# Two fused image layers on one core: half of the first image's sums by 32 x 32 block transposes, a new scratch layout, and output products on tiles of 32 rows and 64 columns

## The chip, the cores and the metric

The kernel runs on one core of a Trainium2 chip. The metric is the device time of one execution, in microseconds (us); the runs before the change are summed up by their median.

## The reference

The input x has 8 images of 256 channels and 96 x 96 pixels, fp32. Two layers are applied one after the other, each with a residual:

```python
# --- layer 0: attention over channels, in the frequency domain ---
x = x + L0(_gn(x))
#   q, k, v = fft2(1x1 conv of _gn(x)), 8 heads of 32 channels
#   attn = q_normalized . k_normalized * temperature      (over all frequencies)
#   out = |ifft2((softmax(real attn) + i softmax(imag attn)) . v)|, then a 1x1 conv
# --- layer 1: linear attention over pixels ---
x = x + L1(_gn(x))
#   q = softplus(Wq x + bq), k = softplus(Wk x + bk), v = Wv x + bv
#   out = q . (k v^T) / (q . sum k)
```

Sums over all frequencies of products of two transforms are sums over pixels, so the kernel never transforms whole images: it needs the channel covariance of each image with itself and with its mirror image (row -h, column -w), and a rotated copy of the image for the imaginary part.

## The kernel before, in words

One program works on the 8 images one after the other, as generators that are interleaved by hand: each `yield` is a place where another generator may put its instructions, and within each engine the order of the program is the order of execution (`tc.manual_schedule`). Two SBUF arenas hold the current image x (`x_of(b)`) and its rotated copy y (`y_of(b)`); the next image's x uses the arena of the current y.

Per image b there are these stages:

- **Sums** (`first_sums` for image 0, `pair_sums` for the others). A pair of image rows and its mirrored rows are transposed so that pixels lie on partitions; `pair` makes the sum e and the difference o of the two; `products` multiplies e and o with themselves, 8 matmuls per product step, accumulated in two PSUM tiles `acc`. `first_sums` mirrors rows on ScalarE (`mirrored`, L394), transposes them on PE (`turn`, L410), copies them out of PSUM (L412) and takes 96 pixels of one row per product step: 24 units of two steps, and the middle row. The transposed rows stay in SBUF at hand-chosen `places`. `pair_sums` loads the image with 32 channel groups on partitions (`load_grouped`: DMAs of 192 KB into 32 partitions each), turns 32 x 32 blocks on VectorE (`turn_blocks`, L510), makes e on GpSimd (L537) and o on VectorE or GpSimd (L538), and takes 128 pixels per product step: 12 units of three steps, and the middle row. Its transposed rows are written to the DRAM scratch `xtd` (L515), a group of two units with one DMA; the middle row goes to `xtm`.
- **Attention and rotation** (`attention`, `rotate`, joined by `mix`). `attention` is a long chain of small steps from the covariance to the table mz; `rotate` makes y by products of the transposed rows with a table of shifted sines (`tm`, read from `rx` in DRAM), 49 steps in all, whose matmuls stand at L128 in the helper `in_halves` as `y<-tm,arena`. `fetch` brings a block of transposed rows back from `xtd` (L799), or, for image 0, finds it at its place. `mix` puts one rotation step at each yield of the chain.
- **Images** (`images`): reloads x, applies mz to y (L875), takes squares and roots, projects with wo (L884) and adds to x. Beside it the next image's sums run (`weave`).
- **Layer 1** (`layer1`, `output`). `output` selects the reciprocal denominators (`select`, L1135), multiplies (L1146), makes the output products (L1173) from 32-row slices, adds them to x (L1178 on VectorE; L1181 and L1182 through ScalarE and GpSimd) and stores the image (L1186). Beside it run the end of the next image's sums and its first 16 rotation and chain steps.

All DMAs are issued by SP in program order. The helper that splits a product into two tiles of 64 columns:

```python
def in_halves(out, lhsT, rhs, start, stop):
    for h in halves:
        nc.tensor.matmul(out[h], lhsT=lhsT[:, h], rhs=rhs, start=start, stop=stop, skip_group_check=True)
```

What orders the work around the change: for image 0, `first_sums` runs to its end with table set-up steps (`tables`) put in from its 11th yield and rotation steps from its 16th, then `mix`; for the others `weave` adds up the yields' numbers and takes one step of the sums each time the sum passes 1. Rings bound how far an engine runs ahead: five `ring` tiles for e and o, five PSUM tiles `ps`, three `acc`.

Of the kernel before, what the change touches and what calls it, by code (L numbers as in the profile page):

```python
# [74 lines left out]
def two_layer_kernel(ctx: ExitStack, tc: tile.TileContext, x, w1t, b1, w2t, b2, w3, b3, wot, temp,  # L75
# [58 lines left out]
    TO = 2 * SG + 4  # L134

# [4 lines left out]
    def turned(b):  # L140

        return [x_of(b)[:, c, TO:TO + 2 * NQ * C].rearrange("p (q r n) -> p q r n", q=NQ, r=2) for c in range(2)]
# [70 lines left out]
    def load_small():  # L213
# [16 lines left out]
        for j in range(16):  # L230
            nc.sync.dma_start(out=wo[NH * j:NH * j + NH, 1, :], in_=wo_v[HEAD - j if j else 16])
            if j % 4 == 3:
                yield
# [17 lines left out]
    xtd = dram.tile([2, NG // 2, P, 2 * NQ * C], F32, name="xtd")  # L251
# [89 lines left out]
    def release(key):  # L341
        if next(held.get(key, iter(())), None) is None:
# [4 lines left out]
              *((0, k, o) for k, o in ((0, 1280), (0, 2304), (0, 5888), (0, 6912), (1, 5888), (1, 6912))),  # L347
              *((1, k, 0) for k in range(KC)), *((0, 1, o) for o in (1280, 2304)), *((1, k, o) for o in (8192, 1024, 7168, 2048, 6144, 3072) for k in range(KC))]
# [6 lines left out]
    def first_loads():  # L355

        nc.sync.dma_start(out=t0[:, 0:2 * W], in_=tmat[0, :, W:3 * W])
        x0 = x_of(0)

        def load(lo, hi):  # L360
            nc.sync.dma_start(out=x0[:, :, lo * W:hi * W], in_=x_v[0, :, :, lo * W:hi * W])

        for lo, hi in ((0, 4), (H - 4, H), (4, 8), (H - 8, H - 4), (8, 16), (H - 16, H - 8)):
            load(lo, hi)
        yield
        load(16, 24)
        yield
        for lo in (H - 24, 24, H - 32):
            load(lo, lo + 8)
        yield  # L370
        for t in range(4, NT // 2):
            load(8 * t, 8 * t + 8)
            load(H - 8 * t - 8, H - 8 * t)
        yield

    def first_sums():
# [3 lines left out]
        acc = [acc_tile(f"acc{c}_{b}") for c in range(2)]  # L380
        CB = C + 2
        NU = H // 4
        eos, gs = {}, {}

        xr = x0[:, :, 0:HW].rearrange("p k (h w) -> p k h w", w=W)

        def mirrored(u):

            nr = 2 if u < NU else 1
            g = two.tile([P, CH], F32, tag="v16", name=f"g_{b}_{u}")[:, 0:KC * nr * W].rearrange("p (k r w) -> p k r w", k=KC, r=nr)  # L390
            h = H - 2 * u
            parts = [(g, xr[:, :, h:h - nr:-1])] if u else [(g[:, :, r:r + 1], xr[:, :, (H - r) % H:(H - r) % H + 1]) for r in range(nr)]
# [5 lines left out]
        def turn(u):  # L398

            t = place(u)  # L400
            nr = 2 if u < NU else 1
            g = gs.pop(u)
            if u < NU:
                gs[u + 1] = mirrored(u + 1)
            for c in range(2):
                pt = ps_tile(f"x_{b}_{u}_{c}")
                for r in range(nr):
                    for k in range(KC):
                        v = g[:, k, r, :] if c else xr[:, k, 2 * u + r, :]
# [4 lines left out]
        def pair(u):  # L414

            nr = 2 if u < NU else 1
            eo = ring_tile(f"eo_{b}_{u}")[0:W, 0:2 * nr * CB].rearrange("p (q c n) -> p q c n", q=nr, c=2)
            f, g = (place(u)[:, c * N2:c * N2 + nr * C].rearrange("p (r n) -> p r n", r=nr) for c in range(2))
            e, o = (eo[:, :, c, 1:C + 1] for c in range(2))
            nc.gpsimd.memset(eo[:, :, :, 0:CB:CB - 1], 1.0 if u < NU else R2)  # L420
            if u in (0, NU):
# [5 lines left out]
            if u < NU:  # L427
                nc.gpsimd.tensor_add(e, f, g)
                nc.vector.tensor_sub(o, f, g)
# [7 lines left out]
        for u in range(NU + 1):  # L437
            if u + 2 <= NU:
                turn(u + 2)
            if u < NU:  # L440
                pair(u + 1)
            eo = eos.pop(u)
            for q in range(2 if u < NU else 1):
                products(acc, eo, q, W, u == 0 and q == 0, u == NU)
            yield
        s0[b] = acc, weights(b)
# [25 lines left out]
    def pair_sums(b):  # L472

        ready = {}

        def prepare(key, step):
            if key in (("turn", 10), ("pair", 10), ("turn", 11), ("turn", 12)):
# [8 lines left out]
        acc = [acc_tile(f"acc{c}_{b}") for c in range(2)]  # L486
# [4 lines left out]
        def turn_blocks(u):  # L491

            v, r = divmod(u, 2)
            t = turned(b)
# [19 lines left out]
            if r:  # L514
                nc.sync.dma_start(out=xtd[:, v].rearrange("c p m -> p c m"), in_=x_of(b)[:, :, TO:TO + 2 * NQ * C])  # L515
# [3 lines left out]
        def pair(u):  # L519
# [3 lines left out]
            ft, gt = (t[0:np_, 0:nq, u % 2] for t in turned(b))  # L523
# [17 lines left out]
        finish(turn_blocks(0))  # L541
        finish(make(0))
        finish(turn_blocks(1))
        if b:
            finish(make(1))
        yield
        for u in range(NG + 1):
# [15 lines left out]
    def attention(b):  # L563
# [37 lines left out]
        nmean, rstd, dm = yield from group_norm(mv, f"a{b}", 1)  # L601
# [4 lines left out]
        yield 4  # L606
# [152 lines left out]
    def rotate(b):  # L759
# [5 lines left out]
        def load_r(i):  # L765
# [3 lines left out]
            if b == 0 and i < NP:  # L769
# [8 lines left out]
        assert LO + 16 * C <= AW and LO + 12 * C <= LO + NS * CH + 2 * CH  # L778
        xts, tms = {}, {}
        at_ = [0]  # L780

        def fetch():
# [8 lines left out]
            if b == 0:  # L791
# [5 lines left out]
            else:  # L797
                v, a = divmod(i, G)
                nc.sync.dma_start(out=xts[i], in_=xtd[:, v, 32 * a:32 * a + 32].rearrange("c j (q m) -> (j q) c m", q=NQ))  # L799
# [34 lines left out]
    def images(b):  # L834
# [100 lines left out]
        for p in pending:  # L935
            yield 1
            project(*p)
# [4 lines left out]
    def layer1(b):  # L942
# [4 lines left out]
        nmean, rstd, _ = yield from group_norm(mv, f"b{b}")  # L947
# [182 lines left out]
    def output(b, x, kq, rec, am, columns_of, fetch=None, sums=None, mixed=None):  # L1130

        def select(s, pd, half=2):
            t, g = divmod(s, 4)
            n = slice(CH // 2 if half == 1 else 0, CH if half else CH // 2)
            nc.tensor.matmul(pd[:, n], lhsT=sel8[32 * g:32 * g + 32, t * P:(t + 1) * P], rhs=rec[32 * g:32 * g + 32, n],  # L1135
                             start=True, stop=True, skip_group_check=True)
# [30 lines left out]
        for s in range(NS):  # L1167
            for m in range(KC):
                po = []
                for j in range(NB):  # L1170
                    ps = ps_tile(f"o_{b}_{s}_{m}_{j}")
                    jj = slice(32 * j, 32 * j + 32)
                    nc.tensor.matmul(ps[:, 0:CH], lhsT=am[jj, m * P:(m + 1) * P], rhs=qn(s)[jj], start=True, stop=True)  # L1173
# [26 lines left out]
    def mix(b, chain, turns):  # L1200

        for n in chain:
            for _ in range(n):
                next(turns, None)
                yield
# [6 lines left out]
    with tc.manual_schedule(engines={E.PE, E.DVE, E.Pool, E.SP, E.Activation}):  # L1212
        sums, loads, parts = first_sums(), first_loads(), tables()
# [8 lines left out]
        for i, _ in enumerate(sums):  # L1222
            if i > 9:
                next(parts, None)
            if i > 14:
                next(turns)
        finish(mix(0, attention(0), turns))
# [61 lines left out]
```

## Time and profile before

| what | value |
|---|---|
| runs before | 2467.61, 2470.61, 2471.26 us; median 2470.61 |
| profiled execution | 2469.41 us, of which the span of instructions 2467.6 us |
| PE matmul busy | 2385.8 us (97%), granted clock 0.983 of full |
| PE weight loads busy | 1492.3 us (60%) |
| VectorE (DVE), ScalarE (ACT), GpSimd (POOL) busy | 1782.0 us (72%), 1162.1 us (47%), 864.7 us (35%) |
| DMA | 395.26 MB, mean 160 GB/s; 53.7% of 16 engines' span |

How to read it: busy times are shares of one profiled execution. A row of a group of instructions names the line, the engine, the operation, what it writes and reads, the shape, the count, busy us and mean ns of one, then the engine's idle time just before them and what ended it. Matmuls are pipelined, so a busy PE is not PE at its peak. An fp32 product appears in the trace as two matmuls (two passes), each with its weight load; a transpose as one. A DMA share of 1 means that all 16 engines had a packet in work all the time. Stretches are given as start:end in us from the start of the span.

### The profile page before, as it was taken

The page shows a single profiled execution, that of the slowest core. Times are in us where ns is not written, and L with a number is a line of the kernel's source. Part 1 is how long each engine was busy: PE and PEld are TensorE (multiplying, and loading weights), DVE is VectorE, ACT ScalarE, POOL GpSimd, SP SyncE. Part 2 cuts the span into 40 slices and gives each one's busy share as a digit, 9 for nine tenths or more (in the row PEclk, how much of TensorE's full clock was granted, in tenths as well). Part 3 has the DMA queues.
Part 4 walks back from the last instruction along what each step waited for, and adds up shares of the span by engine and source line. Part 5 has one row for each costly group of instructions (what it writes and reads, how often), then busy time and mean ns, then how long its engine had stood idle before and what let it go on. Part 6 is the DMA issues. An engine that isn't in the chain of part 4 may idle for free. (4 is left out here: it accounts for less than half of the span.)

```text
span 2467.6 us, 60810 instructions
## 1 busy us (share of the span) xinstructions
PE 2385.8 (97%) x25296; PEld 1492.3 (60%) x25296; DVE 1782.0 (72%) x3472; ACT 1162.1 (47%) x2053; POOL 864.7 (35%) x820
## 2 busy tenths in 40 slices
PE   9999998999989999899999999989999999999998
PEld 7854666456774566645666456664666546665446
DVE  4478785688857887578775787757886578866777
ACT  3354354544535445354453535435364453644553
POOL 4124513344213543135331352413524136142311
PEclk9999999999999999899999999999999999999997
DMA  8135729266391755916559263783638737296004
GB/s 234 41 130 128 190 78 329 106 164 155 129 335 53 175 139 167 333 34 160 135 196 316 53 171 96 251 260 65 167 88 297 214 65 200 54 329 207 1 8 154
DMA packets 264718, 395.26 MB, mean 160 GB/s; under 512 B 37400, under 2 KB 194300, under 8 KB 264444
## 3 DMA queue, kind: packets, MB, share of 16 engines
q1 hardware_dynamic: 264444, 391.38, 53.7%
q8 instruction: 200, 3.28, 0.6%
q14 instruction: 74, 0.61, 0.1%
HBM read 246.99 MB, written 144.32 MB: 159 GB/s over the span
## 5 line engine op out<-in xcount | busy, mean ns | idle before, releaser
L875 PE MATMUL z<-arena,mz 128*64 128x384 f32 (+1 forms) x3840 | 594.9, 489 | 0.0
L927 POOL TENSOR_TENSOR e<-e 128x768 f32<-128x768 f32 x192 | 349.7, 1821 | 533.7 <-ACT e L926 507.7
L884 PE MATMUL po<-e,wo 128*64 128x384 f32 x3072 | 529.4, 486 | 1.8 <-ACT e L928 1.8
L875 PEld LDWEIGHTS z<-arena,mz 128*64 128x64 f32 (+1 forms) x3840 | 247.5, 132 | 296.6 <-issue 287.4
L922 DVE TENSOR_TENSOR e<-z,xT 128x768 f32<-128x768 f32 x384 | 359.2, 947 | 43.8 <-PE z L875 43.0
L884 PEld LDWEIGHTS po<-e,wo 128*64 128x64 f32 x3072 | 227.9, 137 | 266.3 <-issue 235.2
L469 PE MATMUL acc<-eo 128*64 128x193 f32 (+6 forms) x4928 | 379.5, 303 | 0.8 <-DVE eo L425 0.4
L469 PEld LDWEIGHTS acc<-eo 128*64 128x64 f32 (+1 forms) x4928 | 327.3, 136 | 81.4 <-issue 55.5
L926 ACT ACTIVATE e<-e 128x1536 f32<-128x1536 f32 x192 | 284.4, 1481 | 151.2 <-DVE e L922 149.3
L128 PE MATMUL y<-tm,arena 96*64 96x97 f32 x6144 | 316.5, 254 | 37.9 <-issue 18.7
L928 ACT ACTIVATE e<-e 128x768 f32<-128x768 f32 x192 | 162.0, 844 | 383.2 <-POOL e L927 381.2
L128 PEld LDWEIGHTS y<-tm,arena 96*64 96x64 f32 x6144 | 287.1, 140 | 89.0 <-issue 53.6
L886 DVE TENSOR_TENSOR arena<-arena,po 128x384 f32<-128x384 f32 x384 | 208.6, 551 | 160.0 <-PE po L884 159.6
L537 POOL TENSOR_TENSOR eo<-arena 128x768 f32<-128x768 f32 x77 | 157.7, 2049 | 397.5 <-DVE arena L510 305.4
L1182 POOL TENSOR_TENSOR arena<-arena,po 128x384 f32<-128x384 f32 x180 | 180.5, 1022 | 182.9 <-ACT po L1181 179.7
L819 ACT COPY arena<-y 128x384 f32<-128x384 f32 (+1 forms) x200 | 94.7, 475 | 219.8 <-PE y L128 207.3
L303 DVE BATCH_NORM_STATS2 st<-arena 128x6 f32<-128x384 f32 x384 | 195.2, 548 | 0.6
L819 DVE COPY arena<-y 128x384 f32<-128x384 f32 (+1 forms) x192 | 104.4, 544 | 125.5 <-PE y L128 124.4
L510 DVE STREAM_TRANSPOSE arena<-arena 128x768 f32<-128x768 f32 x168 | 155.1, 955 | 15.9 <-DMA xtd<-arena 14.8
L1181 ACT COPY po<-o 128x384 f32<-128x384 f32 x180 | 79.3, 481 | 184.0 <-PE o L1173 182.1
L1042 PE MATMUL xT<-ident,arena 128*128 128x128 f32 x1152 | 144.1, 275 | 1.3 <-ACT xT L1045 1.3
L1042 PEld LDWEIGHTS xT<-ident,arena 128*128 128x128 f32 x1152 | 127.1, 141 | 19.0 <-issue 16.5
(247 smaller groups left out, 2589.3 us busy)
## 6 DMA issues: line engine op xcount, KB each, us to landing
arena<-in_x_dram SPq DMA_DIRECT2D x106, 768.0 KB
out_dram<-arena SPq DMA_DIRECT2D x192, 384.0 KB
xtd<-arena SPq DMA_DIRECT2D x42, 1536.0 KB
arena<-xtd SPq DMA_DIRECT2D x168, 384.0 KB
arena<-in_x_dram SPq DMA_DIRECT2D x329, 192.0 KB
tm<-rx SPq DMA_DIRECT2D x96, 159.0 KB
wl<-in_w1t_dram SPq DMA_DIRECT2D x8, 256.0 KB
wl<-in_w2t_dram SPq DMA_DIRECT2D x8, 256.0 KB
```

What stands on the lines that cost most here:

```text
L128: nc.tensor.matmul(out[h], lhsT=lhsT[:, h], rhs=rhs, start=start, stop=stop, skip_group_check=True)
L303: nc.vector.bn_stats(out=st[:, k, c, :], in_=x_of(b)[:, k, c * CH:(c + 1) * CH])
L469: nc.tensor.matmul(o, lhsT=v[:, 1 + m * HP:1 + (m + 1) * HP], rhs=of, start=(first and m < 2), stop=last, skip_group_check=True)
L819: copy(y[:, :, :, g:g + nr, :], v.rearrange("p k r (f w) -> p k f r w", f=2))
L875: nc.tensor.matmul(out[:, 0:CH].rearrange("p (h q) -> p h q", q=PR), lhsT=columns(mz, k, c, j)[:, h], rhs=yz[:, k, f, :, o:o + PR], start= ...
L884: nc.tensor.matmul(po[h, 0:CH], lhsT=wo[:, k, m * P:(m + 1) * P][:, h], rhs=e[:, k, :], start=(k == 0), stop=(k == KC - 1), skip_group_che ...
L886: nc.vector.tensor_add(x[:, m, n], x[:, m, n], po[:, 0:CH])
L922: nc.vector.tensor_add(e[:, 2 * c:2 * c + 2, :].rearrange("p t (q h) -> p t q h", h=H), pz[:, 0:CH].rearrange("p (h q) -> p q h", h=H).uns ...
L926: nc.scalar.activation(e, e, AF.Square)
L927: nc.gpsimd.tensor_add(e[:, 0:2, :], e[:, 0:2, :], e[:, 2:4, :])
L1042: nc.tensor.transpose(pt[:, j * C + k * P:j * C + (k + 1) * P], x[:, k, o:o + P], ident)
L1182: nc.gpsimd.tensor_add(x[:, m, r], x[:, m, r], t)
```

## The change

Image 0: `first_sums` makes 12 units (rows 0 to 23 and their mirror rows) in place of 24 and the middle row; its row loads stop there, and rows 0 to 23 go to another part of the arena. `pair_sums(0)` then continues with units 6 to 12 into the same accumulators, its first four steps beside the last four units of `first_sums`. Its groups 3 to 5 and the middle row go through `xtd` and `xtm`; the turned rows of group 4 lie in the other arena (`turned_flat`). The rotation of image 0 takes blocks 0 to 11 from their places and 12 to 24 from the scratch, through five slots. Table set-up steps come later, and the wo rows one per step.

Scratch: `xtd` holds for each pixel both kinds of rows, the plain and the mirrored, side by side: a group is written with two DMAs, a block read as 96 rows of 4 KB.

All images: `select` and the output products go through `in_halves`; one product step moves from between the last two projections to before the group norm of layer 1 (yields 0, 1 and 3 in place of 1, 1 and 2); in `attention`, one rotation step moves from after the group norm to before it (2 and 3 in place of 1 and 4). The diff, cut to its core:

```diff
+    TO2 = 7040
+    V0 = 3
...
-    def turned(b):
+    def turned_flat(b, u):
-        return [x_of(b)[:, c, TO:TO + 2 * NQ * C].rearrange("p (q r n) -> p q r n", q=NQ, r=2) for c in range(2)]
+        if b == 0 and u // 2 == V0 + 1:
+            return y_of(b)[:, :, TO2:TO2 + 2 * NQ * C]
+        return x_of(b)[:, :, TO:TO + 2 * NQ * C]
+
+    def turned(b, u):
+        t = turned_flat(b, u)
+        return [t[:, c].rearrange("p (q r n) -> p q r n", q=NQ, r=2) for c in range(2)]
...
-    xtd = dram.tile([2, NG // 2, P, 2 * NQ * C], F32, name="xtd")
+    xtd = dram.tile([NG // 2, P, NQ, 2, 2 * C], F32, name="xtd")
...
+    NU = V0 * G
...
-        load(16, 24)
+        load(16, 2 * NU)
         yield
-        for lo in (H - 24, 24, H - 32):
-            load(lo, lo + 8)
+        load(H - 2 * NU + 1, H - 16)
+        load_grouped(0, V0)
         yield
-        for t in range(4, NT // 2):
-            load(8 * t, 8 * t + 8)
-            load(H - 8 * t - 8, H - 8 * t)
+        load_grouped(0, V0 + 1)
         yield
...
-        for u in range(NU + 1):
-            if u + 2 <= NU:
+        for u in range(NU):
+            if u + 2 < NU:
                 turn(u + 2)
-            if u < NU:
+            if u + 1 < NU:
                 pair(u + 1)
             eo = eos.pop(u)
-            for q in range(2 if u < NU else 1):
-                products(acc, eo, q, W, u == 0 and q == 0, u == NU)
+            for q in range(2):
+                products(acc, eo, q, W, u == 0 and q == 0, False)
             yield
...
+        u0 = 0 if b else 2 * V0
...
-                nc.sync.dma_start(out=xtd[:, v].rearrange("c p m -> p c m"), in_=x_of(b)[:, :, TO:TO + 2 * NQ * C])
+                for c in range(2):
+                    nc.sync.dma_start(out=xtd[v][:, :, c], in_=turned_flat(b, u)[:, c].rearrange("p (q m) -> p q m", q=NQ))
...
-        nmean, rstd, dm = yield from group_norm(mv, f"a{b}", 1)
+        nmean, rstd, dm = yield from group_norm(mv, f"a{b}", 2)
...
-        yield 4
+        yield 3
...
-                nc.sync.dma_start(out=xts[i], in_=xtd[:, v, 32 * a:32 * a + 32].rearrange("c j (q m) -> (j q) c m", q=NQ))
+                nc.sync.dma_start(out=xts[i].rearrange("p c m -> p (c m)"), in_=xtd[v, 32 * a:32 * a + 32].rearrange("j q c m -> (j q) (c m)"))
...
-        for p in pending:
-            yield 1
+        for n, p in enumerate(pending):
+            yield n
             project(*p)
...
-        nmean, rstd, _ = yield from group_norm(mv, f"b{b}")
+        nmean, rstd, _ = yield from group_norm(mv, f"b{b}", 3)
...
-            nc.tensor.matmul(pd[:, n], lhsT=sel8[32 * g:32 * g + 32, t * P:(t + 1) * P], rhs=rec[32 * g:32 * g + 32, n],
-                             start=True, stop=True, skip_group_check=True)
+            in_halves(pd[:, n], lhsT=sel8[32 * g:32 * g + 32, t * P:(t + 1) * P], rhs=rec[32 * g:32 * g + 32, n],
+                      start=True, stop=True)
...
-                    nc.tensor.matmul(ps[:, 0:CH], lhsT=am[jj, m * P:(m + 1) * P], rhs=qn(s)[jj], start=True, stop=True)
+                    in_halves(ps[:, 0:CH], lhsT=am[jj, m * P:(m + 1) * P], rhs=qn(s)[jj], start=True, stop=True)
...
-        sums, loads, parts = first_sums(), first_loads(), tables()
+        sums, rest, loads, parts = first_sums(), pair_sums(0), first_loads(), tables()
...
         for i, _ in enumerate(sums):
-            if i > 9:
-                next(parts, None)
-            if i > 14:
-                next(turns)
-        finish(mix(0, attention(0), turns))
+            if NU - 5 < i < NU:
+                next(rest)
+        for i, _ in enumerate(rest):
+            if i == 0:
+                for _ in range(4):
+                    fetch()
+            if i > 12:
+                next(parts, None)
+            for _ in range(2 if i in (9, 10, 11) else 1 if i > 11 else 0):
+                next(turns)
+        finish(mix(0, attention(0), turns, parts))
+        finish(parts)
```

## The prediction

> **What bounds the kernel now.** I read the page first, then the groups with shapes kept apart, the PE timeline of the first 100 us, the busy time by stretch, and the trace's packet records (sizes and times). The page:
>
> ```profile
> PE 2385.8 (97%) x25296; PEld 1492.3 (60%) x25296; DVE 1782.0 (72%) x3472; ACT 1162.1 (47%) x2053; POOL 864.7 (35%) x820
> ...
> DMA  8135729266391755916559263783638737296004
> ```
>
> PE is the engine to relieve nearly everywhere, but the DMA row peaks once per image. The PE timeline of image 0's sums (start, us, engine, line, operation):
>
> ```profile
> 17.03 0.64 PE L410 MATMUL x<-ident,arena 128*96 128x128 f32 x4
> 17.51 0.60 PE L410 MATMUL x<-ident,g 128*96 128x128 f32 x4
> 18.04 2.42 PE L469 MATMUL acc<-eo 96*64 96x193 f32 x32
> 20.39 0.64 PE L410 MATMUL x<-ident,arena 128*96 128x128 f32 x4
> ```
>
> From start to start: 1.01 us of transposes (18.04 - 17.03), 2.35 us of products (20.39 - 18.04), 3.36 us per unit, and no idle time is noted. Two of the unit's image rows are two product steps, so a step of 16 matmuls costs 1.17 us.
>
> Busy time by stretch; the first row is these sums, the second the rest of image 0's first stage, the third and fourth image 0's output stage and what follows it (rotation of image 1), the last the output of image 7. After the engines come PEclk, DMA share and GB/s:
>
> ```profile
> 13.68:90.60 76.92, 76.92 (x978) 66.44 (x978) 32.81 (x70) 24.42 (x70) 34.06 (x46) 1.00 0.52 141
> 95.50:135.46 39.96, 39.63 (x765) 34.11 (x762) 26.37 (x92) 17.96 (x59) 1.24 (x9) 1.00 0.31 109
> 362.00:391.70 29.70, 28.70 (x383) 18.28 (x378) 20.36 (x55) 15.77 (x42) 21.72 (x23) 1.00 1.04 347
> 391.70:435.25 43.55, 36.85 (x655) 31.89 (x655) 22.56 (x72) 14.57 (x49) 3.17 (x11) 0.96 1.06 316
> 2437.60:2461.00 23.40, 23.40 (x100) 18.74 (x100) 19.46 (x40) 5.27 (x11) 10.38 (x11) 0.56 0.88 326
> ```
>
> The reader is to see two regimes. In image 0's sums PE is full and DMA half idle. From the output of an image to the end of the next one's rotation the DMA engines are full (1.04, 1.06) and PE idles 6.7 of 43.6 us. The same stretch before the six later images leaves PE idle 6.7, 6.4, 5.2, 7.6, 5.9 and 3.5 us, 42 us over all seven, at DMA share 1.06 each time: there the transfers set the end.
>
> The output products of line 1173:
>
> ```profile
> 372.30 1.76 PE L1173 MATMUL o<-xT,own 32*128 32x384 f32 x8
> 373.99 1.56 PE L128 MATMUL y<-tm,arena 96*64 96x97 f32 x32
> 375.47 0.93 PE L1173 MATMUL o<-xT,own 32*128 32x384 f32 x8
> 376.33 0.89 PE L128 MATMUL y<-tm,arena 96*64 96x97 f32 x16
> ```
>
> A group of four products takes 0.86 us to the next instruction (375.47 to 376.33) when its four PSUM buffers are free, 1.69 (372.30 to 373.99) when one is late.
>
> **What the Trainium skill says.** "TensorE: Matmul & The Clock Gate", section "Part 3: Packing small matmuls — row/col tiling": tiles in different rows and columns of the array run at once. The trace agrees for four row tiles: eight passes of 384 columns in 0.86 us; no run here shows eight tiles. "TensorEngine Tiling (Array Packing)", "Key Properties": a change of tiling mode drains the array. In the trace, some 0.09 us pass at such a change, also between 128 rows and 2 rows both on 64 columns, so a 32-row tile of 64 columns drains too. "DMA: Bandwidth & Descriptors", "Why small descriptors are slow (HBM only)": a fixed overhead per packet. The packet records agree: medians of 65 ns at 1536 bytes, 84 at 2048, 239 at 6144, a line of 38 ns per KB plus about 8.
>
> **The change part by part.**
>
> *Image 0's sums.* Rows 24 to 72 leave the PE-transposed way. Out go twelve units of 3.36 us and the middle row (0.57 + 1.17): 42.0 us of PE. In come six units of 128 rows with three product steps each, and the middle one: 19 x 1.17 = 22.2 us (a step's time doesn't depend on its rows: 1.17 is also what the 128-row steps of later images take when unbroken, 2.19 us for two). PE gains 19.8 us. What hides the rest:
>
> ```profile
> L537 POOL TENSOR_TENSOR eo<-arena 128x768 f32<-128x768 f32 x77 | 157.7, 2049 | 397.5 <-DVE arena L510 305.4 <-DVE nmean_b L323 48.3 <-issue 40.5
> L510 DVE STREAM_TRANSPOSE arena<-arena 128x768 f32<-128x768 f32 x168 | 155.1, 955 | 15.9 <-DMA xtd<-arena 14.8 <-issue 0.3
> L538 DVE TENSOR_TENSOR eo<-arena 128x768 f32<-128x768 f32 x35 | 33.4, 954 | 15.2 <-POOL eo L525 14.3
> ```
>
> Per unit DVE does two transposes, half a pair of wrap copies (0.593 + 0.578) and a subtraction: 1.91 + 0.59 + 0.95 = 3.45 us against PE's 3.51; POOL 2.05 + 0.12. DVE is a hair under PE, and the first two units are prepared beside the last four old ones, where it has 2 us free in each 3.36. If DVE were shared or late by 20%, six units would lose 0.6 us each: 4 us.
>
> *Its loads.* Eight DMAs of 192 KB for each of two groups replace row loads in SP's queue. By 30 us the engines had moved 8.1 MB before; group 3 completes as about the first 8.1 MB of the new order, and DVE asks for it near 37 us. In between stand the table's rx writes, which SP waits for at 26.7 us; group 4 comes after them, near 45 us by its place, and is asked for near 50. I take 0; up to 8 us if group 3 is late, since DVE's queue would then hold the old units' copies too.
>
> *Image 0's rotation.* 13 column blocks now come from the scratch, not from SBUF: 13 x 1.0 to 1.6 us of all engines in a stretch whose share is 0.31 of 40 us, fetched four blocks ahead. On SP they stand among table loads spread one per step. Three rotation steps move from the attention chain (39 yields, then 36 steps) into the sums, so its last three yields have no filler. I take +1 us for both (0 to +4).
>
> *Scratch layout, images 1 to 7.* A block read is 96 packets of 4096 bytes in place of 192 of 2048; a group's write 768 packets of 2048 in place of 256 of 6144, on two DMAs. Writes: 768 x 84 / 16 = 4.0 us against 256 x 258 / 16 = 4.1, beside PE-bound stages: 0. Reads are in the stretch that DMA bounds. The line gives 163 ns for 4096 bytes against 2 x 84: 24 blocks x 96 x 5 / 16 = 0.7 us per image; scaled to the measured mean (117 ns for 2048) about 1.0. But in the second half of the stretch, reads alone, 2048 bytes take 136 ns: the cause isn't in the trace. If it vanished with whole 4-KB rows, 12 blocks would save 12 x 96 x (272 - 163) / 16 = 7.8 us per image, capped by PE's idle time, 42 us in sum. If rows of 4 KB were slower, see the rival. I take -0.8 x 7 = -5.6 us.
>
> *Output products and the select on 32 x 64 tiles.* Twice the instructions (384 to 768, 80 to 160 in the program). A 128-column first pass starts streaming 0.106 us after its weight load, a 64-column one 0.053 (2-row products of line 128): -0.05 per group; eight tiles are issued some 7 ns apart: +0.03. Of images 0 to 6 DMA hides either. In image 7 DVE, 19.5 of 23.4 us, paces: 0, at best -4 if PE's clock (0.56 there) changed.
>
> *Sum step and yields.* One product step moves from between image b's last two projections to before its group norm, and one rotation step to before the other norm.
>
> ```profile
> L128 PE MATMUL gm_b<-mv_b,gavg_sb 128*64 128x2 f32 x32 | 2.3, 209 | 5.7 <-DVE mv_b L309 5.7
> L128 PE MATMUL gv_b<-dv_b,gavg_sb 128*64 128x2 f32 x32 | 2.4, 214 | 3.2 <-ACT dv_b L321 3.2
> ```
>
> The first wait, 5.7 us over eight images, is covered. But the step brings a subtraction (0.95) into DVE's queue ahead of dm, beside the 1.9 of transposes already there, and gv_b waits for dm: the wait moves on. Worth 0 (-0.7 to +0.3 per image); who waits is PE with all its products.
>
> *Sum:* -19.8 + 1 - 5.6 = -24.4, from the profiled 2469.41 (span 2467.6 and 1.8 around it) 2445.0. The median, 2470.61, is 1.2 above, so 2446.
>
> **The rivals.** (1) *Reads are freed.* For: the 136 against 84 ns. Against: bytes and destination partitions are unchanged. With 30 of PE's idle 42 us gone, 2470.6 - 18.8 - 30 = 2422. (2) *The new sums starve* on loads or DVE and keep half: 2470.6 - 9.9 + 1 - 5.6 = 2456. For: 3.45 against 3.51. Against: two prepared units. (3) *Eight tiles run as two fours*: 0.64 us per group, 7.7 per image; PE's idle 6.0 per image hides most, 7 x 1.7 + 7.7 = 20 remains: 2466. Against: 128 x 32 tiles run four at once (85 ns per pass of 384 columns, line 997). (4) *Slower: whole rows read worse.* If 4096 bytes cost 272 ns in all 24 blocks, 38 above today's 2 x 117, that is 24 x 96 / 16 x 38 ns = 5.5 us per image on the transfers that set the end, 38 in all: 2446 + 5.6 + 38 = 2490. It decides from 253 ns per packet (18.8 / 7 / 144 packets per engine). For: no page of the trace explains the 136; against: other sizes follow the line. (5) That the change does nothing can be excluded: 100 transposes and 48 products leave the program.
>
> **How the numbers follow.** Likeliest 0.55 (2446, its own range 2438 to 2454), rival 1 0.18, rival 2 0.11, rival 3 0.06, rival 4 0.10. The range leaves out rival 4 and the lower third of rival 1: 2418 to 2466. Measurement tells 0.2%, 4.9 us, from no change: faster is the likeliest, 1, 2 and a sixth of 3, 0.85; same the rest of 3, 0.05; slower 0.10.
>
> **What would show it.** The PE timeline after 48 us: product steps of 1.17 us back to back, no transposes; image 0's first stage ends near 117 us in place of 135.5. In the stretches at DMA share 1.06, 4096-byte packets near 2 x 117 ns or less, and PE's idle 42 us little changed. I am wrong if PE waits for DVE's transposes or x loads before 75 us, if the output groups take over 1 us with free buffers, or if packets exceed 253 ns.

## The result, and the profile after

| | before | after |
|---|---|---|
| runs on one chip | 2464.02 to 2471.26 us (6) | 2457.24 to 2462.95 us (6) |
| median | 2469.11 us | 2462.06 us |
| profiled execution (its span) | 2469.41 us (2467.6) | 2462.42 us (2460.6) |

The ratio is 0.9967, with a 95% interval of 0.9955 to 0.9978: by it the change takes 8 us off (the medians differ by 7), where 24 were forecast. The page of the profile after, its busy row of PE and its DMA row in 40 slices:

```profile
PE 2358.3 (96%) x26028; PEld 1466.4 (60%) x26028; DVE 1785.2 (73%) x3474; ACT 1148.8 (47%) x2015; POOL 861.1 (35%) x806
...
DMA  9535729275491655926478363873729638295004
```

PE works 27.5 us less (2385.8 - 2358.3), so the removed work is gone. Against the row of before the second digit of the DMA row has risen from 1 to 5, the first from 8 to 9: image 0's first 120 us are where the trace has changed most.

PE's timeline of the changed kernel, image 0's sums and the first rotation steps (start, us, engine, line, operation, then in brackets the idle time before and what ended it):

```profile
49.59 11.15 PE L476 MATMUL acc<-eo 128*64 128x193 f32 x160
64.15 2.21 PE L128 MATMUL y<-tm,arena 96*64 96x97 f32 x24 [3.40 <-DMA tm<-rx]
66.10 2.01 PE L476 MATMUL acc<-eo 128*64 128x193 f32 x16
...
80.59 1.01 PE L128 MATMUL y<-tm,arena 96*64 96x97 f32 x16 [4.06 <-DMA tm<-rx]
81.32 2.43 PE L476 MATMUL acc<-eo 128*64 128x193 f32 x16
...
94.44 2.48 PE L128 MATMUL y<-tm,arena 96*64 96x97 f32 x32 [2.22 <-DVE mv_a L599]
```

The new product steps come back to back as forecast: ten of them (160 matmuls) in 11.15 us. Then PE waits, for table pieces of the rotation and for the covariance, and the first steps after a wait take 2.0 to 2.4 us in place of 1.2. The end of image 0's first stage, its last products (L753), then starts at the same time as before (135.46 there):

```profile
135.45 0.84 PE L753 MATMUL b<-b3col,scr 128*64 128x1 f32 x32
```

So all of image 0's forecast gain is lost in image 0's first stage. The busy time in stretches of 10 us, first one of the kernel before, then those of the changed one (after the engines come PEclk, DMA share, GB/s):

```profile
40.00:50.00 10.00, 10.00 (x124) 8.48 (x122) 6.65 (x24) 3.30 (x9) 4.89 (x8) 1.00 0.67 252
```

```profile
40.00:50.00 10.00, 9.62 (x130) 8.27 (x128) 8.71 (x10) 1.67 (x4) 8.82 (x7) 1.00 0.98 225
50.00:60.00 10.00, 10.00 (x151) 9.73 (x148) 5.86 (x8) 0.00 (x0) 5.76 (x6) 1.00 1.11 278
60.00:70.00 10.00, 6.60 (x95) 6.23 (x93) 3.15 (x5) 1.09 (x4) 2.63 (x2) 0.83 0.74 225
70.00:80.00 10.00, 6.53 (x121) 6.28 (x116) 7.22 (x28) 1.09 (x4) 2.06 (x2) 1.00 0.52 184
80.00:90.00 10.00, 9.41 (x144) 9.37 (x146) 3.49 (x16) 1.40 (x5) 0.00 (x0) 0.83 0.46 107
90.00:100.00 10.00, 7.78 (x123) 7.28 (x121) 4.15 (x14) 2.93 (x10) 0.91 (x3) 0.74 0.50 134
100.00:110.00 10.00, 10.00 (x133) 8.33 (x132) 3.37 (x14) 3.73 (x10) 0.00 (x0) 0.57 0.54 139
```

From 60 to 100 us PE idles 9.7 us (40 less 6.60 + 6.53 + 9.41 + 7.78). Its clock is at half in three stretches up to 110 us, in all of which it is busy:

```profile
64.16:67.58 3.42, 3.42 (x36) 3.28 (x38) 1.30 (x2) 0.00 (x0) 2.63 (x2) 0.50 0.59 170
81.23:84.64 3.41, 3.41 (x37) 3.34 (x35) 0.84 (x2) 0.85 (x3) 0.00 (x0) 0.50 0.13 29
94.88:108.53 13.65, 13.65 (x157) 11.64 (x155) 3.69 (x16) 4.29 (x12) 0.00 (x0) 0.50 0.53 146
```

Half of these 20.5 us, at most, is lost by that. Together the two are about the 18.4 us between the forecast's 117 and 135.4. The DMA engines, which before fell to a share of 0.67 from 40 us and 0.23 from 50 us, now stay at about 1 until 60 us. (A share over 1 means that the recorded times of packets overlap on an engine.)

Three more things stand as forecast. In the stretches from an image's output to its successor's rotation PE still idles 39.8 us in sum (before 42) at nearly the same DMA share (1.04 or 1.05, before 1.06), here the first of seven:

```profile
389.60:431.20 41.60, 37.05 (x673) 31.15 (x657) 22.79 (x71) 14.71 (x49) 2.60 (x10) 0.96 1.04 322
```

The scratch's 4096-byte packets take 222 ns in the mean, under the 234 of two former ones. And a group of output products, now 16 matmuls on eight tiles, takes 0.83 us to the next instruction (373.57 to 374.40) where four tiles took 0.86:

```profile
373.57 0.90 PE L128 MATMUL o<-xT,own 32*64 32x384 f32 x16
374.40 0.89 PE L128 MATMUL y<-tm,arena 96*64 96x97 f32 x16
```

### The profile page after: what moved, and what is told of

It is laid out like the page before. It is cut to its first block, busy times and chain, and to the rows that moved or that the text cites. A ratio compares the mean times of both kernels' runs of the same rounds, so it can differ in the third digit from the quotient of the medians.

```text
span 2460.6 us, 62299 instructions
## 1 busy us (share of the span) xinstructions
PE 2358.3 (96%) x26028; PEld 1466.4 (60%) x26028; DVE 1785.2 (73%) x3474; ACT 1148.8 (47%) x2015; POOL 861.1 (35%) x806
## 5 line engine op out<-in xcount | busy, mean ns | idle before, releaser
L128 PE MATMUL y<-tm,arena 96*64 96x97 f32 x6144 | 321.6, 258 | 59.0 <-DMA arena<-xtd 24.3
L476 PEld LDWEIGHTS acc<-eo 128*64 128x64 f32 (+1 forms) x4448 | 302.9, 136 | 68.9 <-issue 49.2
L476 PE MATMUL acc<-eo 128*64 128x193 f32 (+4 forms) x4448 | 342.2, 303 | 0.0
L546 POOL TENSOR_TENSOR eo<-arena 128x768 f32<-128x768 f32 x83 | 172.9, 2084 | 412.5 <-DVE arena L518 355.9
L518 DVE STREAM_TRANSPOSE arena<-arena 128x768 f32<-128x768 f32 x180 | 166.6, 956 | 2.2 <-DMA xtd<-arena 0.8
```

Source lines behind the costliest of these rows:

```text
L476: nc.tensor.matmul(o, lhsT=v[:, 1 + m * HP:1 + (m + 1) * HP], rhs=of, start=(first and m < 2), stop=last, skip_group_check=True)
```

## Where image 0's time goes: two readings

SP's timeline of the changed kernel (issues of DMAs; lines left out are loads):

```profile
46.44 1.38 SPq L524 DMA_DIRECT2D xtd<-arena  x2
47.87 1.31 SPq L169 DMA_DIRECT2D arena<-in_x_dram  x1
...
56.08 1.76 SPq L780 DMA_DIRECT2D tm<-rx  x2
58.01 1.52 SPq L524 DMA_DIRECT2D xtd<-arena  x2
...
71.47 1.38 SPq L524 DMA_DIRECT2D xtd<-arena  x2
72.90 2.59 SPq L780 DMA_DIRECT2D tm<-rx  x2
```

And VectorE's, its waits:

```profile
50.92 0.18 DVE L513 COPY wrap<-arena 128x16 f32<-128x16 f32 x1 [2.21 <-DMA arena<-in_x_dram]
...
62.28 0.17 DVE L513 COPY wrap<-arena 128x16 f32<-128x16 f32 x1 [5.26 <-DMA arena<-in_x_dram]
...
70.13 0.36 DVE L831 COPY arena<-y 128x192 f32<-128x192 f32 x1 [4.57 <-DMA xtd<-arena]
```

A chain can be read here. Group 5's loads (L169, L171) are issued from 47.87 us, behind group 3's scratch write, and VectorE waits for them until 62.28. Group 4's write, issued at 58.01, lands near 70: VectorE's first rotation copy waits for it, because the turned rows of group 4 lie where the rotation writes. Group 5's write therefore comes at 71.47, and the next two table pieces stand behind it; PE waits for those until 80.59.

The first two pieces, issued at 56.08 behind group 5's loads, are what PE waits for until 64.15. Up to then the DMA engines are full; later they aren't. While VectorE waits for group 4's write, and when group 5's is about to start, they have room (columns as in the stretches above):

```profile
65.00:70.00 5.00, 5.00 (x77) 4.85 (x75) 0.57 (x1) 1.09 (x4) 2.28 (x2) 0.74 0.43 109
71.00:72.00 1.00, 1.00 (x26) 1.00 (x24) 1.00 (x2) 0.54 (x2) 0.00 (x0) 1.00 0.00 0
```

*Theory A, the order:* the table pieces and loads are late because SP holds them behind writes that wait for VectorE. *Theory C, the load:* they are late because the DMA engines are full. The packet records summed over the first 62 us, in us of 16 engines (own sum of count x mean time / 16):

```
packets                          before    after
x loads by rows (1536 to 3072 B)   25.9     13.3
x loads by groups (768 B)           0.5     24.9
scratch writes (2048 B)               -      5.3
table reads (384 B)                12.1     12.3
table writes and pieces (1696 B)    8.2      7.2
others                              3.2      1.7
sum                                49.9     64.7
```

The same bytes of x cost twice the time by groups: a packet of 768 bytes takes 63 ns in the mean here, one of 3072 took 131 before. And image 0, which wrote nothing to the scratch before, now writes 3 groups of 768 packets.

## The experiments

The kernel before was run beside each; ratios are to it. "Stage end" is the start of L753's products of image 0 in the profile (before 135.46, after 135.45). Changes of a run's stage end are read from one profile each. What follows varies more: the stretch from image 4's stage end to image 5's took 297.4 to 305.4 us in the profiles of kernels that differ from the changed one in image 0 alone. So for images 1 to 7 only medians speak.

**Parts of the change.** Three kernels take one part each. `layout_alone` is before with the new form of the scratch, `tiles_alone` before with the two kinds of products through `in_halves`, and `mixed_alone` the changed kernel with old form, old products and old yields:

```diff
 layout_alone, on before
-    xtd = dram.tile([2, NG // 2, P, 2 * NQ * C], F32, name="xtd")
+    xtd = dram.tile([NG // 2, P, NQ, 2, 2 * C], F32, name="xtd")
...
 tiles_alone, on before
...
-                    nc.tensor.matmul(ps[:, 0:CH], lhsT=am[jj, m * P:(m + 1) * P], rhs=qn(s)[jj], start=True, stop=True)
+                    in_halves(ps[:, 0:CH], lhsT=am[jj, m * P:(m + 1) * P], rhs=qn(s)[jj], start=True, stop=True)
```

Expected of `layout_alone`:

> The kernel before with only the scratch layout of the change (two writes per group, reads of whole 4-KB rows). Theory A (the 1.1 us per image that images 1 to 7 gained come from the reads: 4096-byte packets take a mean of 222 ns where two of 2048 took 234, 144 per engine and image, 1.7 us): 1 to 1.7 us per image, 2457 to 2463 us. Theory C (they come from the output products on smaller tiles or the moved steps): 2467 to 2471 us.

Expected of `tiles_alone`:

> The kernel before with only the select and the output products on tiles of 32 rows and 64 columns. Theory A (a group becomes 0.03 us shorter, 0.86 to 0.83, and in images 0 to 6 the transfers hide that): 0 to 3 us, 2466 to 2470 us. Theory C (shorter groups let stores start earlier, and so the transfers that bound the stage): 5 to 8 us, 2461 to 2464 us.

Expected of `mixed_alone`:

> The changed kernel with the old scratch layout, the old output tiles and the old yields: only image 0's sums are changed. Theory A (the first stage gains nothing because of the late table pieces, and later images don't depend on it): within 2 us of before, 2467 to 2471 us, and image 0's first stage ends near 135 us. Theory C (the time gained by the changed kernel comes from image 0 in some other way): 2461 to 2464 us.

Measured: the layout 2459.26 us, ratio 0.9971 (0.996 to 0.9981); the tiles 2470.06, 1.0003 (0.999 to 1.0016); the mixed sums 2467.48, 1.0003 (0.9989 to 1.0017). The layout alone gives 7.2 us, which is the whole of the change within the intervals. The mixed sums, for which 18.8 us were forecast, give nothing. In the one profile of that kernel image 0's stage ends at 130.51, 5 us earlier than before the change or after it; the medians show nothing of it, and whether image 0 loses less with the old scratch (the same bytes in a third of the packets) stays open.

**The table pieces ahead** (`tm_early`): on the changed kernel, the first four pieces are fetched before group 3's write.

```diff
+            if i == NU - 5:
+                for _ in range(8):
+                    fetch()
             if NU - 5 < i < NU:
                 next(rest)
...
-            if i == 0:
-                for _ in range(4):
-                    fetch()
```

> The changed kernel with one thing moved: the first four pieces of the rotation table (tm) are issued before the scratch writes and the loads of group 5 of image 0, instead of after them. Theory A (the gain of image 0's sums was lost because the table pieces stand behind the scratch writes, which wait for VectorE, and behind grouped loads, so that PE waits 3.4 and 4.1 us and then runs at a reduced clock): the two waits go, 7.5 us, and with them a part of the slow clock, worth up to 10 us; 2445 to 2455 us, image 0's first stage ends at 119 to 128 us instead of 135.5. Theory B (VectorE and the grouped loads of image 0 are late by themselves, and PE would only wait for them instead): less than 3 us, 2459 to 2463 us, with PE waiting for VectorE or GpSimd near 65 to 82 us.

Measured 2455.28 us, 0.9954 (0.9934 to 0.9974); stage end 130.33. The wait for the table falls to 1.8 us in the first stage. But group 5's loads, now behind the pieces, land at 71 in place of 62 us (VectorE waits 14.6 us for them), and PE waits 8.0 us for the copies that stand behind on VectorE and ScalarE:

```profile
71.19 0.17 DVE L513 COPY wrap<-arena 128x16 f32<-128x16 f32 x1 [14.59 <-DMA arena<-in_x_dram]
```

Under the changed kernel that is 3 us by the ratios, 7 by the medians, of the up to 17 that theory A asked for. The wait has moved rather than gone.

**Group 5's loads ahead** (`g5_early`), and both (`g5_tm_early`): group 5 gets a place in the other arena, so that its loads follow group 4's.

```diff
+        if b == 0 and v == V0 + 2:
+            return y_of(b)[:, 1, at * SG:at * SG + SG + at]
...
         load_grouped(0, V0 + 1)
+        load_grouped(0, V0 + 2)
...
```

> The changed kernel, but image 0's sixth group of rows (72 to 80 and their mirrors) gets a place of its own in the other arena, so that its eight loads are issued with those of the fifth group and not behind the fourth group's scratch write. Theory A (image 0's gain is lost to two things that stand on SP's queue behind a scratch write which waits for VectorE: the sixth group's loads, for which VectorE and then TensorE wait, and the table pieces of the rotation, which stand behind those loads): the loads leave the place ahead of the table pieces too, so both come about 8 us earlier; image 0's first stage ends near 122 to 127 us in place of 135.5, and the time is 2448 to 2454. Theory B (the DMA engines are full until 60 us, so what comes earlier only pushes something else later; or TensorE's lowered clock between 60 and 110 us is the loss and not its consequence): 2459 to 2464.

> Both at once: the sixth group's loads with those of the fifth, and the first four table pieces of the rotation fetched ahead of the fourth group's scratch write. Theory A: no wait for either is left, the first stage ends near 118 to 123 us, TensorE's clock stays at 1.0, and the time is 2443 to 2450, at or under the record's forecast of 2446. If only the sixth group's loads were late, as the table pieces already come earlier with them, this is within 2 us of the run with the loads alone. Theory B: no better than the tables alone, 2453 to 2457.

(Both count the groups from one: the sixth is group 5 of the code.) Measured: 2455.37 us, 0.9952 (0.9935 to 0.997), stage end 132.34, between the ranges of the two theories; both together 2462.58 us, 0.9975 (0.9963 to 0.9986), stage end 138.15, which neither had. The loads, issued from 45.1 us on and not from 47.9, landed at 58.6, 3.7 us earlier than without this edit, where 8 were expected; the writes and table pieces, now behind them, came later, and VectorE waited 4.4 us for a write again:

```profile
58.62 0.94 DVE L516 COPY wrap<-arena 128x16 f32<-128x16 f32 x1 [0.78 <-DMA arena<-in_x_dram]
...
69.18 0.36 DVE L835 COPY arena<-y 128x192 f32<-128x192 f32 x1 [4.42 <-DMA xtd<-arena]
```

With both edits group 3's write stands behind everything and lands at 70 us, and VectorE waits 9.9 us for it. Theory A, which made the two together the best, is wrong as it was put: each order delays another transfer.

**No scratch for image 0** (`no_scratch0`): image 0 neither writes nor reads it, and its rotation takes other rows, which lie in SBUF, in place of 13 blocks. **Larger packets** (`big_packets0`): image 0's groups are filled by runs of 6144 bytes (other data of the image, the same bytes), to take load off the engines. And both.

```diff
 no_scratch0
...
-                for c in range(2):
+                for c in range(2 if b else 0):
                     nc.sync.dma_start(out=xtd[v][:, :, c], in_=turned_flat(b, u)[:, c].rearrange("p (q m) -> p q m", q=NQ))
...
-            if b == 0 and i < NU:
-                xts[i] = place(i).rearrange("p (c m) -> p c m", c=2)
+            if b == 0:
+                xts[i] = place(i % NU).rearrange("p (c m) -> p c m", c=2)
...
 big_packets0
+            if b == 0:
+                xb = x[b].rearrange("c h w -> c (h w)")[32 * a:32 * a + 32]
+                nc.sync.dma_start(out=f[s].rearrange("p c w -> p (c w)"), in_=xb[:, h * W:h * W + SG])
...
```

> The changed kernel, but image 0 neither writes nor reads the scratch: its three grouped blocks are not written, and the rotation takes other rows from SBUF in their place (image 0's output is another one; work of the engines unchanged). Theory A: the writes that stand ahead of the loads and the table pieces on SP's queue are gone, as are VectorE's waits for them: 2446 to 2452. Theory C: the writes are only 5.3 of the 59.1 us of packets before 62 us; the sixth group still lands after 56 us: a part comes back, 2452 to 2458.

> The changed kernel, but image 0's three grouped loads fetch the same number of bytes into the same places as runs of 6144 bytes (8 channels' worth of one channel's rows) in place of runs of 768: image 0's data are other ones, the work and the order on every queue are unchanged. Theory C (image 0's first 60 us are bound by the DMA engines: the packets up to 62 us sum to 59.1 us of 16 engines, of which the 768-byte packets of the grouped loads take 24.9, and everything issued after 45 us lands 8 to 12 us late because of it): the grouped loads' packets fall to under 8 us in sum, no wait of VectorE for group loads is left, the table pieces land within 4 us, the first stage ends near 119 to 123 us, and the time is 2445 to 2451. Theory A (the order on SP's queue, scratch writes that wait for VectorE ahead of the loads and the table pieces): the order is unchanged, so most of the loss stays: 2457 to 2462.

> Both of the edits: image 0's grouped loads in runs of 6144 bytes, and no scratch for image 0. Theory C: with neither load on the DMA engines, TensorE has no wait over 2 us between 48 us and the end of the first stage, its clock stays at 1.0, the stage ends near 117 us as the record has it, and the time is 2442 to 2447. If the loss had another cause, such as VectorE or GpSimd being too slow for the grouped way or TensorE's clock, it stays above 2452.

(The 59.1 us in the first two texts were added up wrongly: the packets sum to 64.7, as in the table above.)

Measured: without the scratch 2444.14 us, 0.9904 (0.9885 to 0.9923), stage end 120.89. That is under the ranges of both theories, 2 us from theory A's and 8 from theory C's. PE's waits in the first 140 us are of 1.9 us at most apart from the start-up's 3.6, and PE's clock is 1.00 up to 110 us:

```profile
PE pcs L266 <- POOL xo L431: 3.6, 1, 3.6
PE y L128 <- ACT ys L833: 1.9, 1, 1.9
```

This is the record's forecast, 2446, reached by leaving one thing out: image 0's scratch costs 15.5 us by the ratios and 18 by the medians, with a stage end 14.6 us earlier, and 16 us were missed. The loads by groups are all still there, so by themselves they cost little. VectorE and GpSimd keep up with PE in the grouped way.

The larger packets failed as an experiment: 2482.9 us, 1.0056 (1.0036 to 1.0077), and with no scratch 2474.46, 1.003 (1.0018 to 1.0041). The edit brought a wait of its own: ScalarE's mirrored copies (L408) came to wait for the grouped loads, until 34.3 us, and PE for them (its longest wait up to 140 us, here in the kernel with the scratch):

```profile
PE x L424 <- ACT g L409: 27.1, 1, 27.1
```

One thing can be read from the pair: in these two kernels the DMA engines stand at a share of 0.01 from 50 to 70 us, and with the scratch PE still waits 10.4 us for table pieces afterwards (the engines are full again at 80 to 90 us, at 1.02), without it none. So the scratch costs image 0 much of the same when the first loads have long landed: 8.4 us by the medians (2482.9 - 2474.46), 10.6 by the stage ends (157.93 and 147.29). A backlog from the first 45 us isn't needed for it.

**What of the scratch costs.** `no_reads0` keeps the writes and takes the blocks from SBUF; `thin_no_reads0` in addition cuts each row that is written to 256 bytes, at the same number of packets, with the same order of waits and places on SP's queue. (Only its edit of the writes is shown.)

```diff
 thin_no_reads0
+                m = 2 * C if b else C // 4
                 for c in range(2):
-                    nc.sync.dma_start(out=xtd[v][:, :, c], in_=turned_flat(b, u)[:, c].rearrange("p (q m) -> p q m", q=NQ))
+                    nc.sync.dma_start(out=xtd[v][:, :, c, 0:m], in_=turned_flat(b, u)[:, c].rearrange("p (q m) -> p q m", q=NQ)[:, :, 0:m])
```

> The changed kernel, but image 0's rotation takes its last 13 column blocks from SBUF (other rows) and not from the scratch, whose writes stay. If the 13 block reads stand in the rotation's way, as part of the 18 us that image 0 gained without the scratch: 2450 or less. If they are hidden, as the record's +1 us has it (0 to +4), and all is lost on the writing side: 2458 to 2462.

> As the run without block reads, but image 0's scratch writes carry an eighth of each row (256 bytes in place of 2048; packets, issues and the waits for VectorE as before). Theory C (the bytes of the writes delay what stands behind them on full DMA engines): 2444 to 2449, as without the scratch. Theory A (SP's order and the waits at the writes cost the time, whatever the writes carry): 2454 to 2460. Between the two if the delay is the time from issue to landing, for which VectorE's next transposes and its copies of the rotation wait.

Measured: without reads 2461.6 us, 0.997 (0.9958 to 0.9981), stage end 133.42: the reads cost nothing that shows. With thin writes 2449.24 us, 0.9924 (0.991 to 0.9939), stage end 118.72, within 2 us of the forecast's 117. The time lies 0.2 us above theory C's range (2444 to 2449) and 5 us under theory A's. PE's waits between 44 and 122 us, without reads and then with thin writes:

```profile
PE y L128 <- DMA tm<-rx: 7.4, 2, 4.1
PE y L128 <- DVE scr L595: 1.9, 1, 1.9
```

```profile
PE y L128 <- DVE ss L594: 1.0, 1, 1.0
...
PE y L128 <- DMA tm<-rx: 0.2, 1, 0.2
```

The order on the queue, what waits for what and the number of packets are those of the changed kernel, and only the bytes are fewer; the 7.4 us for table pieces become 0.2. So it is the bytes of the three writes that cost image 0 most of its gain: 12.4 us between the two medians (2461.6 - 2449.24), 14.7 between the stage ends. From 44 to 70 us the 2048-byte packets take 8.4 us of 16 engines (1536 of them at 88 ns), the 256-byte ones 2.9 us (2304 at 20 ns). Fewer bytes take less of the engines, and each write also lands sooner after its issue: VectorE goes on with its rotation copies at 62.5 us in place of 69.6. The run doesn't part these two. In PE's clock the difference shows too; one stretch without reads, then with thin writes:

```profile
90.00:100.00 10.00, 8.13 (x128) 7.63 (x125) 4.91 (x18) 2.77 (x11) 0.91 (x3) 0.72 0.35 92
```

```profile
90.00:100.00 10.00, 9.97 (x153) 7.97 (x155) 7.00 (x20) 4.15 (x13) 0.00 (x0) 1.00 0.17 48
```

The 5 us between thin writes and no scratch aren't in image 0 (118.72 against 120.89), and the two intervals overlap.

**Only the waits around the writes** (`act_copies_tm0`, and `g5_act_copies_tm0` with group 5's loads ahead): the first eight rotation copies all on ScalarE, and four table pieces where two were.

```diff
-            copy = (nc.scalar.copy, nc.vector.tensor_copy)[i % 2]
+            copy = (nc.scalar.copy, nc.vector.tensor_copy)[i % 2 if b or i > 7 else 0]
...
             if i == 0:
-                for _ in range(4):
+                for _ in range(8):
                     fetch()
```

> The changed kernel with image 0's first eight rotation copies all on ScalarE, so that VectorE's transposes of the last group don't stand behind a copy that waits for the fifth group's scratch write, and four table pieces fetched where two were, ahead of that write. Theory W (one write of 12 us from issue to landing holds VectorE, which holds the last write, behind which the next table pieces stand): 4.6 us of VectorE's wait and 4.1 us of TensorE's go, and the time is 2452 to 2456. If full DMA engines are the cause whatever the order: 2459 to 2463.

> The same with the sixth group's loads issued with the fifth's. Theory W: the sixth group lands near 58.5 us as in the earlier run of that edit, no copy holds VectorE, and only the third group's write has to land before its transposes: 2447 to 2453, the best version with everything computed. If full DMA engines are the cause: 2455 to 2460, no better than either edit alone.

Measured: 2458.76 us, 0.9959 (0.9944 to 0.9975), stage end 133.19; and 2464.41, 0.9987 (0.9976 to 0.9998), stage end 135.86. Neither meets theory W. VectorE is free of the write and has turned the last blocks by 67.7, but group 5's write is issued at 71.8 all the same, since SP is issuing the middle row's six loads from 63.0 to 71.3, and PE waits 8.5 us for table pieces. In the second, VectorE's last transposes wait 9.2 us for copies on ScalarE, which wait in VectorE's place (for an x load and the write, by the profile). The other reading, full engines, named the direction and not the size: the first lies just under its range, the second 4 us above its range and above the changed kernel.

## Why the prediction was wrong

**Right.** A product step takes 1.1 us from 49.59 us on, and VectorE and GpSimd hardly bound it: with thin writes the stage ends at 118.72 against 117 forecast. (The forecast's 1.17 doesn't fit the 2.19 us for two that it quotes beside it; with 1.1 the removed work is 21 us and not 19.8.) The output products on eight tiles: 0.83 us per group, the forecast's change of -0.02 to -0.03, and nothing in the time (1.0003). Rivals 1, 3 and 4 are out: PE's idle 42 us became 39.8, a group didn't go to two fours, and a packet of 4096 bytes takes 222 ns, short of 253. Yields and the moved sum step weren't run by themselves; what the three parts and the whole leave for them is about 1 us (8.2 less 7.2), within the intervals.

**The layout, right in the time.** Forecast 5.6 us, measured 7.2 (4.7 to 9.9). Over images 1 to 7 the reads' packets went from 236.8 to 222.3 us of 16 engines in `layout_alone`, 2.1 us per image where the forecast had 0.8. The writes went the other way, from 178.2 to 200.4 us, 4.8 per group against the forecast's 4.0 (its 84 ns for 2048 bytes is the commonest time; the median of all such packets before is 120); as the time fell all the same, nothing of this shows, as the forecast said. That the shorter reads bring the 7 us is argued. The stretches from an image's last output products to the end of the next one's rotation sum to 300.8 us before, 287.3 in `layout_alone` and 299.7 after, one profile each, which is too uneven to show it.

**Wrong: "Image 0's rotation", +1 us.** This is the step that failed. It priced the 13 block reads, which cost nothing that shows, and not the three group writes that must come first, nor what waits for them to land. It put the forecast's own price, 4.0 us of 16 engines for a group of 768 packets, only on images 1 to 7, where it doesn't show; for image 0 it stands at nothing. The runs put the cost of these bytes at 2461.6 - 2449.2 = 12.4 us and that of image 0's whole scratch at 15.5 to 18, where 16 us were missed. Part of it is the engines' time for the writes (3 x 4.0 us by the forecast's price), part the chain behind them: group 4's write lands 12 us after its issue, VectorE's copies wait for it, group 5's write for VectorE, two table pieces for that, and PE for these. How the loss divides between the two isn't shown.

**Incomplete: the step "Its loads", with "I take 0".** It asked in which order image 0's transfers stand on SP's queue and when VectorE asks for groups 3 and 4. Group 3 was not late, and group 4's lateness of 2.2 us was covered. It left out group 5, whose loads come behind group 3's write and ahead of the first table pieces, and for which VectorE waits 5.3 us. And it didn't sum packet times against the time in which they must be done. By the forecast's own numbers, half the image in packets of 768 bytes is 6144 of them. At the mean of 62 ns that the records of before show for this size this is 24 us of 16 engines, against 13 us by rows. The DMA share of 0.52 that the forecast quoted for 13.68 to 90.6 us is a mean over 1.08 from 10 to 20 us and 0.01 from 80 to 90. Still, without the scratch the same loads come to the forecast time, so the 0 for them stands only as long as no writes are added.

**Rival 2, "starve on loads or DVE and keep half",** named the right place and the wrong extent. Late transfers cost twice: the waits themselves, 9.7 us, and a lowered PE clock after them. The Trainium skill, "TensorE: Matmul & The Clock Gate", section "Part 1: The HAM clock gate (the "warmup" mystery)", says that the clock falls to half after an idle window of about 3.4 us and comes back after as long a busy one. The trace agrees after the waits of 3.40 and 4.06 us: the clock is at 0.50 for 3.42 and 3.41 us, and the product steps that follow take 2.01 and 2.43 us in place of 1.29. It doesn't agree from 94.88 to 108.53 us: there the half clock follows a wait of 2.22 us and stays for 13.65, though PE is busy throughout. Here the measurement decides, and the runs give no cause.

**The order of the queue** was the first theory after the result and is not the cause by itself: with the order kept and thinner writes most of the loss is gone. The skill's "DMA: Bandwidth & Descriptors", section "Issuing engines are not separate DMA queues", says that all transfers run on the same 16 engines, whichever engine starts them. Here SP starts them all; that they share a limit shows in the runs in another way: whichever of table pieces, group 5's loads and group 3's write was put first, another landed late, at 71 us for the loads, at 70 for the write.

`tm_early` and `g5_early` compute everything and were the fastest such kernels, at 2455.3 and 2455.4 us; their intervals overlap with that of the change, so that a gain from them isn't established. No version that computes everything came near the forecast, and none was tried that writes less for image 0 before 70 us.

## What to carry to other kernels

Before work is moved to a way that loads earlier or in smaller pieces, sum the packet times of everything that must land before the point of need, the new writes included, and hold the sum against the time there is; a mean DMA share over a longer stretch hides a full first half. A scratch write that is free in one stage isn't free in a start-up where loads, table pieces and other engines' work stand behind it: ask what waits for it to land. Each of the five other orders tried here made another transfer late, and none came near the forecast. To tell bytes from the order, keep every issue and wait and thin the bytes alone.

## What the runs showed of the hardware that was not expected

- A load of 192 KB as 32 runs of 6144 bytes over 32 partitions took 441 ns per packet in the mean (median 473), where scratch writes of the same size took 265 in the kernel before: larger packets gained less than their size promised (14.1 us of 16 engines for the 512 packets of groups 3 and 4, where packets of 768 bytes, 4096 of them at 63 ns, take 16.1).
- The same 2048-byte size took 117 ns in the mean as block reads in the kernel before and 99 as writes in the changed one.
- A write issued at 58.0 to 59.5 us released VectorE's copy at 70.1, over 10 us later, though the engines were full only until about 64 us (a share of 0.43 from 65 to 70); with an eighth of the bytes the issue at 55.1 to 56.6 was landed by 62.0.
- PE's clock stood at half for 13.65 us of uninterrupted work after a wait of 2.22 us (changed kernel), and for 3.41 us after one of 1.9 us (`no_scratch0`, from 115.65).
